# V of an attention layer by 20 products with 171-column blocks in place of seven Strassen products

## The chip, the core and the metric

One Trainium2 chip, one of its cores. The time is device microseconds of one launch of the whole program; the time of a kernel is the median of several runs.

## What is computed

The input `x` is 128 graphs of 128 nodes with 512 features, in f32. Layer 0 mixes the nodes of each graph by `adj`, takes a row maximum, adds it to `x` and normalises. Layer 1 is masked attention with 8 heads of 64 columns, a projection, and two normalisations. What matters here is the part of layer 1 ahead of the attention:

```python
def _L1_gnn_ref(x, w_qkv, w_proj, b_proj, ln_gamma, ln_beta, attn_mask):
    ...
    qkv = (x @ w_qkv).reshape(b, n, 3, H, hd).transpose(2, 0, 3, 1, 4)
    q, k, v = (qkv[0], qkv[1], qkv[2])
    attn = jnp.einsum('bhnd,bhmd->bhnm', q, k) * scale
    attn = jnp.where(attn_mask[None, None] == 0, -jnp.inf, attn)
    attn = jax.nn.softmax(attn, axis=-1)
    o = jnp.einsum('bhnm,bhmd->bhnd', attn, v).transpose(0, 2, 1, 3).reshape(b, n, d)
    o = o @ w_proj + b_proj
    ...
```

So V is `x` (all tokens by 512) times the last 512 columns of `w_qkv` (512 by 512), and everything stays in f32.

## The kernel before

**Groups and steps.** Four graphs make a group, 512 tokens; there are 32 groups and one step of the main loop (L1353) for each. The step of group p attends the group before (A: `attend`, L1153), forms scores and softmax of group p (S: L1030 and L1049), V of group p (V), the projection of group p-1 (O: `o_unit`, L1001), layer 0 of group p+2 (L: `l0_mm`, L474), and Q and K of group p+1 (Q: `Bilinear`, L799). The order of TensorE's pieces in a step is written out by hand in three lists: `FIRST` (L140) for the first step, `STEP` (L134) for the 30 in the middle, `LAST` (L146) for the last. `V5` in a list is product 5 of V, `Q17` is node 17 of Q and K, and so on. In the first step I, J, X and D stand for layer 0 of groups 0 and 1, transposes on TensorE, and Q and K of group 0 by plain products (`qk_plain`, L745). In the last step B, T and R attend, finish and project what is left.

**The other engines.** Every piece of work is an `Op` with a cost, an engine and the buffers it reads and writes. `Plan.run` (L212) keeps TensorE's order as the lists have it, and sorts the work of VectorE (DVE), ScalarE (ACT), GpSimd (POOL) and the DMA queue of SyncE (SP) by the time at which TensorE will want it. Each engine then executes its own queue strictly in that order.

**Q and K** are not formed by plain products. `token_sums` (L777) makes 18 sums of the eight token blocks `x1T` (each 128 features by 256 tokens) on POOL, into nine buffers `hl0` to `hl8`. `weight_forms` (L683) makes 26 sums of blocks of the weights once, at the start, on DVE and ACT. `Bilinear.node` (L823) walks a table: a node adds one or two products into a PSUM bank, and the bank is then handed on to a later node (chain), copied by ACT into another bank that a later node goes on with (a seed, L844), copied by ACT to an SBUF buffer `u` for later use (L847), or combined on DVE, and on POOL for a second summand, into a block of the result. One product of Q and K is two matmuls that stream 256 columns, and each f32 matmul is two MATMUL instructions in the profile.

**V and the projection** use Strassen's method with seven products on 2 by 2 blocks (`Strassen`, L901). A product is four matmuls of 256 columns, that is eight MATMUL instructions in the profile; seven products are 56. For V, `v_unit` (L967) makes four token sums on POOL per group (`unit_sums`, L985, into `hl0` to `hl3`), takes three ACT copies of the accumulating bank (`snap`, L936) and four DVE additions that write the result (`result`, L938). The weights of V need four sums on POOL at the start (`weight_sums(wv)`, L1418).

**PSUM** has eight banks, handed out first in, first out (`take`, L358).

The three places where the list sets V among the rest are these:

```python
STEP = """
A0 A1 A2 A3 S0 S1 S2 S3 V1 V2 L0 L1 V6 V5 O1 O2 V7 L3 L2 V4 O6 V3 O5 O7 O4 Q0 O3 Q2 Q3 Q1 Q4 Q5 Q6
Q7 Q8 Q9 Q10 Q11 Q12 Q13 Q14 Q15 Q17 Q16 Q19 Q20 Q18 Q21 Q22 Q24 Q25 Q23
""".split()
LAST = """
A0 A1 S0 A2 S1 A3 V1 S2 S3 O1 V5 V6 V4 O5 O2 V7 O6 O7 O4 T3 V3 V2 B0 B1 O3 T2 T1 T0 R0 R1 B2 B3 R3
R2
""".split()
```

Of the kernel before, what the change touches and what calls it, by code (L numbers as in the profile page):

```python
# [14 lines left out]
AX = mybir.AxisListType  # L15

# [24 lines left out]
TEMPS = [  # L41
    (10, 13, 1),
    (3, 10, 1),
    (0, 3, -1),
    (4, 7, -1),
    (4, 5, 1),
    (13, 14, -1),
    (9, 17, -1),
    (2, 3, 1),
    (11, 16, 1),  # L50
]
FORMS = [
    ((10, -1), (14, -1)),
    ((19, -1),),
    ((16, 1),),
    ((4, -1), (16, 1)),
    ((3, -1),),
    ((4, -1), (17, 1)),
    ((13, -1),),
    ((3, 1), (12, 1), (16, 1)),  # L60
    ((19, 1), (21, -1)),
    ((17, -1),),
    ((16, -1), (18, 1)),
    ((2, 1), (10, -1)),
    ((12, -1), (24, -1)),
    ((10, 1), (11, 1)),
    ((6, 1), (7, 1), (23, -1)),
    ((0, 1), (22, 1)),
    ((12, 1), (15, -1), (21, 1)),
    ((8, -1), (11, 1), (18, 1)),  # L70
    ((20, -1), (23, 1)),
    ((9, -1), (10, 1)),
    ((15, -1), (19, 1), (24, -1)),
    ((20, -1),),
    ((1, 1), (2, -1), (18, 1)),
    ((1, 1), (20, -1), (22, -1)),
    ((5, 1), (6, -1), (21, 1)),
    ((8, -1), (9, -1), (12, -1), (13, -1)),
]


NODES = [
    (((8, 0),), 3, (2,), (), None),
    (((12, 1),), 6, (), (19,), None),
    (((14, 2),), 4, (8,), (), None),
    (((1, 3), (10, 4)), 5, (), (7,), None),
    (((5, 5), (15, 6)), 9, (7,), (), None),
    (((9, 7),), 25, (10,), (), None),
    (((11, 8),), 14, (12,), (), None),
    (((17, 9),), 11, (20,), (), None),  # L90
    (((13, 10),), 13, (), (16,), None),
    (((16, 11),), 17, (), (12,), None),
    (((18, 12),), 19, (), (11,), None),
    (((19, 13),), 16, (), (15,), None),
    (((5, 14),), None, (), (), 6),
    (((20, 15),), 23, (18,), (), None),
    (((7, 16),), 15, (), (19,), None),
    ((), None, (), (), 7),
    (((6, 17),), None, (), (), 4),
    (((21, 18),), 21, (), (24,), None),  # L100
    (((22, 19),), 22, (), (25,), None),
    (((23, 20),), None, (), (), 3),
    (((24, 21),), 24, (), (22,), None),
    (((0, 22),), None, (), (23, 22), None),
    ((), None, (), (), 1),
    (((25, 23),), None, (), (), 5),
    (((1, 24),), None, (), (), 2),
    (((2, 25),), None, (), (), 0),
]
SIGN = [1, 1, 1, -1, -1, -1, -1, -1, 1, 1, -1, -1, 1, 1, -1, -1, -1, 1, 1, -1, -1, 1, -1, -1, -1, -1]  # L110

EDGES = {
    0: {3: -1, 2: 1},
    1: {19: 1, 6: -1},
    2: {8: 1, 4: -1},
    3: {7: -1, 5: 1},
    4: {7: 1, 9: -1},
    5: {10: 1, 25: 1},
    6: {12: -1, 14: 1},
    7: {11: 1, 20: 1},  # L120
    8: {16: 1, 13: 1},
    9: {12: 1, 17: 1},
    10: {19: 1, 11: 1},
    11: {16: 1, 15: 1},
    13: {18: 1, 23: -1},
    14: {19: 1, 15: 1},
    17: {24: 1, 21: 1},
    18: {25: 1, 22: -1},
    20: {24: 1, 22: 1},
    21: {23: 1, 22: 1},  # L130
}
# [3 lines left out]
A0 A1 A2 A3 S0 S1 S2 S3 V1 V2 L0 L1 V6 V5 O1 O2 V7 L3 L2 V4 O6 V3 O5 O7 O4 Q0 O3 Q2 Q3 Q1 Q4 Q5 Q6  # L135
Q7 Q8 Q9 Q10 Q11 Q12 Q13 Q14 Q15 Q17 Q16 Q19 Q20 Q18 Q21 Q22 Q24 Q25 Q23
# [4 lines left out]
K1 I0 K1 I1 I2 J0 K1 J1 I3 X0 X1 J2 D0 X2 D1 J3 X3 D3 D2 D6 D4 S1 S0 D5 D7 V1 V4 L0 L1 S3 V6 V5 L2  # L141
V7 V2 V3 Q0 Q1 S2 L3 Q2 Q3 Q4 Q5 Q8 Q9 Q6 Q17 Q10 Q7 Q12 Q14 Q21 Q13 Q11 Q19 Q20 Q23 Q18 Q15 Q24 Q25
Q16 Q22
# [3 lines left out]
A0 A1 S0 A2 S1 A3 V1 S2 S3 O1 V5 V6 V4 O5 O2 V7 O6 O7 O4 T3 V3 V2 B0 B1 O3 T2 T1 T0 R0 R1 B2 B3 R3  # L147
R2
# [162 lines left out]
def kernel(  # L311
# [19 lines left out]
    HE = D // 2  # L331
    NG = B // G
# [23 lines left out]
    free = deque(range(8))  # L356

    def take():  # L358
        return bank(free.popleft())
# [319 lines left out]
    def block(i):  # L679
        k, n = divmod(i, 4)  # L680
        return raw[n], None, lambda: raw[n].t[:, k]

    def weight_forms():  # L683
        made = {}
        temp_bufs = [buf(s, [P, 4, HE]) for s in ("z", "xr0", "xr1")]

        def operand(i):
            if i < 16:
                return block(i)
            i -= 16  # L690
            b, c = temp_bufs[i // 4], i % 4
            return b, c, lambda: b.t[:, c]

        def add(dst, dst_at, a, b, sa, sb_):
            (ba, ka, pa), (bb, kb, pb) = a, b
            reads = [(ba, ka), (bb, kb)]
            if sa < 0 and sb_ < 0:
                plan.add(
                    "DVE",
                    0.62,  # L700
                    lambda: stt(dst(), pa(), -1.0, pb(), ALU.mult, ALU.subtract),
                    reads,
                    [dst_at],
                    both=True,
                )
                return
# [3 lines left out]
            plan.add("DVE", 0.49, lambda: tt(V, dst(), pa(), pb(), op), reads, [dst_at], both=True)  # L710

        def temp(i):
            if i in made:
                return
            made[i] = True
            a, b, s = TEMPS[i]
            for o in (a, b):
                if o >= 16:
                    temp(o - 16)
            bt, c = temp_bufs[i // 4], i % 4  # L720
            add(lambda: bt.t[:, c], (bt, c), operand(a), operand(b), 1, s)

        for w, terms in enumerate(FORMS):
            for i, _ in terms:
                if i >= 16:
                    temp(i - 16)
            form, at = (lambda w=w: wqk.t[:, w]), (wqk, w)
# [14 lines left out]
            for i, s in terms[2:]:  # L742
                add(form, at, (wqk, w, form), operand(i), 1, s)
# [55 lines left out]
    class Bilinear:  # L799


        def __init__(self, g):
            self.g, self.left = g, lefts.pop(g)
            self.rooms = deque(f"u{i}" for i in range(6))
            self.banks, self.snaps = {}, {}

        def product(self, b, tok, w, start):
            bt, key, ap = self.left[tok]

            def emit():  # L810
                for s in range(2):
                    mm(halves(b)[:, s], wqk.t[:, w, ts(s, P)], ap(), start and s == 0)

            plan.add("PE", 0.862, emit, [(wqk, w), (bt, key)], [b])

        def place(self, block):
            h, c = divmod(block, 4)
            if (self.g, h) not in qk:
                qk[self.g, h] = buf(f"qk{h}", [P, 4, 2, HT])
            dst = qk[self.g, h]  # L820
            return dst, c, lambda: dst.t[:, c].rearrange("p k n -> p (k n)")

        def node(self, n):  # L823
            prods, chain, seeds, adds, block = NODES[n]
            fresh = n not in self.banks
            b = take() if fresh else self.banks.pop(n)
# [4 lines left out]
            for y in [y for y in self.snaps if n in self.snaps[y][1]]:  # L831
                u, users = self.snaps[y]
                users.discard(n)
                mine.append((u, SIGN[n] * EDGES[y][n] * SIGN[y]))
# [3 lines left out]
            if block is None:  # L838
                for u, s in mine:
                    op = ALU.add if s > 0 else ALU.subtract  # L840
                    plan.add("DVE", 0.62, lambda u=u, op=op: tt(V, b.t, b.t, u.t, op), [u, b], [b])
                for m in seeds:
                    nb = self.banks[m] = take()
                    plan.add("ACT", 0.5, lambda nb=nb: pin(A.copy(nb.t, b.t)), [b], [nb])  # L844
# [626 lines left out]
```

## Time and profile before

| what | value |
|---|---|
| median of 3 runs | 1882.04 us (1880.76 to 1882.06) |
| the profiled execution's own time | 1882.49 us |
| its span, first to last instruction | 1879.6 us |
| busy: TensorE matmul (PE) | 1863.4 us, 11293 instructions |
| busy: TensorE weight load (PEld) | 1594.2 us |
| busy: DVE, ACT, POOL | 1323.9, 1475.6, 1542.1 us |
| DMA | 341.88 MB, mean 182 GB/s |

The profile lists for each engine how long it was busy. A matmul stands in it twice, as a weight load (LDWEIGHTS on PEld) and as a MATMUL on PE; successive MATMULs overlap in the records, so the distance from one start to the next is the cost of one and not its duration. In the timeline and the groups "k" is a PSUM bank, "wv" and "wqk" are the weights of V and of Q and K, "wp" those of the projection, "hl" and "x1T" token sums and token blocks, "so" the token sums of the projection, "u" the copies. A number in brackets at the end of a timeline row is the time for which the engine stood idle before it, with what released it.

### The profile page before, as it was taken

To read this page: it belongs to the slowest core of one execution; us is meant where nothing else is said; L and a number is where in the kernel's file an instruction comes from. 1 tells how busy PE (TensorE), PEld (TensorE's weight loads), DVE (VectorE), ACT (ScalarE), POOL (GpSimd) and SP (SyncE) were. 2 spreads that over 40 slices of the span, in tenths; PEclk is the share of its full clock that TensorE was granted. 3 is DMA by queue.
4 is the path that set the end of the run, shared out by engine and by line. 5 is a ranking of instruction groups with operands and counts; after the bars stand their busy time and mean duration, and the time that the engine had idled before them with its cause. 6 is when DMAs were issued, how large, how long until landed. Compare 5 with 4: busy or idle time off the path is not lost.

```text
span 1879.6 us, 35324 instructions
## 1 busy us (share of the span) xinstructions
PE 1863.4 (99%) x11293; PEld 1594.2 (85%) x11293; DVE 1323.9 (70%) x2433; ACT 1475.6 (79%) x4376; POOL 1542.1 (82%) x1598
## 2 busy tenths in 40 slices
PE   9999999999999999999999999999999999999997
PEld 7788888888888888888888888888888888888884
DVE  8977676676766677667767667676677676677667
ACT  2787777987778877779777788777887777987785
POOL 5678988889888889888898888888888988889884
PEclk9999999999999999999999999999999999999999
DMA  7764676556676556766566765667655677656654
GB/s 220 198 169 128 188 194 198 171 168 182 180 217 181 165 168 189 203 189 171 168 188 183 220 167 167 168 189 214 184 167 165 190 192 196 173 172 177 180 191 146
DMA packets 444888, 341.88 MB, mean 182 GB/s; under 512 B 276768, under 2 KB 378272, under 8 KB 444704
## 3 DMA queue, kind: packets, MB, share of 16 engines
q1 hardware_dynamic: 444416, 339.11, 63.9%
q8 instruction: 90, 1.47, 0.3%
q14 instruction: 94, 0.77, 0.1%
q10 hardware_dynamic: 288, 0.52, 0.1%
HBM read 172.82 MB, written 166.72 MB: 181 GB/s over the span
## 4 chain that ended last, share of the span: by engine, by line
PE 96%; DVE 2%; POOL 1%; issue 0%; ACT 0%; POOLq 0%; DVEq 0%; ACTq 0%
PE k L380 96%; DVE wqk L374 1%; DVE st L497 0%; POOL hl L374 0%; POOL z L374 0%; DVE xr L374 0%; POOL rs L374 0%; DVE z L374 0%; DVE s L377 0%; POOL o L374 0%; DVE qk L771 0%; PE k L642 0%; DVE z L377 0%; DVE nm L1075 0%; POOL wp L374 0%
## 5 line engine op out<-in xcount | busy, mean ns | idle before, releaser
L380 PE MATMUL k<-hl,wqk 128*128 128x256 f32 x2232 | 522.4, 380 | 0.6 <-ACT k L844 0.4
L380 PEld LDWEIGHTS k<-hl,wqk 128*128 128x128 f32 x2232 | 424.6, 190 | 58.7 <-issue 1.2
L1084 ACT ACTIVATE s<-s,nm 128x128 f32<-128x128 f32 x1024 | 395.9, 390 | 7.8 <-DVE nm L1075 7.8
L1113 ACT ACTIVATE s<-s,rec 128x128 f32<-128x128 f32 x992 | 306.3, 391 | 0.0
L377 DVE SCALAR_TENSOR_TENSOR qk<-k,u 128x512 f32<-128x512 f32 x248 | 169.7, 686 | 109.3 <-PE k L380 55.9
L380 PE MATMUL k<-x1T,wqk 128*128 128x256 f32 x992 | 244.5, 380 | 0.0
L374 POOL TENSOR_TENSOR hl<-x1T 128x512 f32<-128x512 f32 (+1 forms) x250 | 216.4, 871 | 33.3 <-PE k L380 33.3
L847 ACT COPY u<-k 128x512 f32<-128x512 f32 x341 | 192.2, 581 | 60.6 <-PE k L380 33.3
L380 PE MATMUL k<-wv,hl 128*128 128x256 f32 x1024 | 237.0, 380 | 1.9 <-POOL hl L374 1.0
L380 PE MATMUL k<-wp,so 128*128 128x256 f32 x992 | 229.7, 380 | 0.7 <-ACT u L936 0.7
L380 PEld LDWEIGHTS k<-wv,hl 128*128 128x128 f32 x1024 | 194.7, 190 | 41.6 <-issue 8.7
L380 PEld LDWEIGHTS k<-wp,so 128*128 128x128 f32 x992 | 188.6, 190 | 26.5 <-ACT u L936 1.1
L380 PEld LDWEIGHTS k<-x1T,wqk 128*128 128x128 f32 x992 | 188.7, 190 | 25.6 <-DVE wqk L374 0.3
L377 DVE SCALAR_TENSOR_TENSOR s<-k,mask 128x512 f32<-128x512 f32 x256 | 156.5, 681 | 72.8 <-PE k L380 72.8
L374 POOL TENSOR_TENSOR hl<-x1T,hl 128x512 f32<-128x512 f32 (+1 forms) x249 | 196.0, 803 | 0.1
L1084 ACT ACTIVATION_READ_ACCUMULATOR s<-s,nm 128x1 f32 x1024 | 193.7, 189 | 0.0
L1125 DVE STREAM_TRANSPOSE pu<-s 128x1024 f32<-128x1024 f32 x128 | 158.2, 1236 | 37.5 <-ACT s L1113 36.4
L380 PE MATMUL k<-wv,x1T 128*128 128x256 f32 x768 | 179.6, 384 | 0.0
L380 PEld LDWEIGHTS k<-wv,x1T 128*128 128x128 f32 x768 | 143.6, 190 | 34.1 <-issue 14.0
L380 PE MATMUL k<-wp,oT 128*128 128x256 f32 x744 | 171.0, 380 | 0.0
L1174 ACT COPY oT<-k 128x512 f32<-128x512 f32 x128 | 75.0, 586 | 118.8 <-PE k L380 118.6
L374 POOL TENSOR_TENSOR x<-x,be_bc 128x1024 f32<-128x1024 f32 x62 | 146.3, 2360 | 19.0 <-ACT xr L568 13.1
(140 smaller groups left out, 3401.7 us busy)
## 6 DMA issues: line engine op xcount, KB each, us to landing
hop<-pu SPq DMA_DIRECT2D x128, 512.0 KB, 2.9
s<-hop SPq DMA_DIRECT2D x512, 128.0 KB, 3.6
xhop<-xt SPq DMA_DIRECT2D x248, 128.0 KB, 3.8
spill<-x SPq DMA_DIRECT2D x62, 512.0 KB, 4.5
x1T<-xhop SPq DMA_DIRECT2D x248, 128.0 KB, 4.6
x<-in_x_dram SPq DMA_DIRECT2D x60, 512.0 KB, 5.0
xr<-spill SPq DMA_DIRECT2D x60, 512.0 KB, 5.1
out_dram<-xr SPq DMA_DIRECT2D x60, 512.0 KB, 4.1
```

The costliest lines, as they stand in the source:

```text
L374: pin(eng.tensor_tensor(dst, a, b, op))
L377: pin(V.scalar_tensor_tensor(dst, a, s, b, op0, op1))
L380: pin(PE.matmul(dst, lhsT=lhsT, rhs=rhs, start=start, stop=True, skip_group_check=True))
L847: plan.add("ACT", 0.5, lambda: pin(A.copy(u.t, b.t)), [b], [u])
L1084: A.activation(flat()[:, i], flat()[:, i], AF.Exp, bias=nm.t[:, i : i + 1], accum_out=sm.t[:, i : i + 1],)
L1113: A.activation(flat()[:, i], flat()[:, i], AF.Identity, scale=rec.t[:, i : i + 1])
L1125: V.transpose(u.t.rearrange("p q h b -> p h q b"), flat().rearrange("p h (q a) -> p h q a", q=Q),)
L1174: lambda: pin(A.copy(dst.t[:, :, ts(jj, P)], bk.t.rearrange("p (c n) -> p c n", c=KC))),
```

## The change

V is formed as Q and K are, from a second table. The result (two blocks of 256 tokens by three blocks of 171 columns, 512 rounded up to 513) is made of 20 products of a token sum and a weight form, in 18 nodes. The token sums are those that `token_sums` made for Q and K of the same group one step earlier; no sums are made for V. The token sum is now the stationary operand and the weight form of 171 columns the one that streams, so a product is two matmuls of 171 columns. The forms of V's weights (8 shared sums, then 20 forms: 12 of one term, 6 of two, 2 of three) are made once, at the start, behind those of Q and K, in the slots of temporary buffers; the raw weights of V lie in the slot of `wp`, so the projection's weights are loaded, and summed on POOL, after V of the first group. V of that first group is formed by plain products (P): four pieces of four matmuls of 512 columns. In the last step the `u` copies of V are made on DVE and not on ACT. The projection is unchanged. All three lists are new.

```diff
+VV = Table(
+    12,
...
+    [
+        (((18, 0),), 4, (3,), (), None),
+        (((21, 1),), 9, (), (8,), None),
+        (((0, 2),), 7, (5,), (), None),
+        (((6, 3),), 6, (), (17,), None),
+        (((7, 4),), 10, (8,), (), None),
+        (((20, 5),), 16, (), (6,), None),
+        (((25, 6),), None, (), (8, 13), None),
+        (((2, 7),), 11, (12,), (), None),
+        (((5, 8),), None, (), (), 4),
+        (((9, 9), (17, 10)), 13, (), (11,), None),
+        (((11, 11),), 15, (14,), (), None),
+        (((24, 12),), None, (), (), 0),
+        (((23, 13),), None, (), (16, 15), None),
+        (((19, 14),), None, (), (), 3),
+        (((14, 15), (13, 16)), 17, (), (16,), None),
+        (((1, 17),), None, (), (), 1),
+        (((22, 18),), None, (), (), 2),
+        (((12, 19),), None, (), (), 5),
+    ],
...
 STEP = """
-A0 A1 A2 A3 S0 S1 S2 S3 V1 V2 L0 L1 V6 V5 O1 O2 V7 L3 L2 V4 O6 V3 O5 O7 O4 Q0 O3 Q2 Q3 Q1 Q4 Q5 Q6
-Q7 Q8 Q9 Q10 Q11 Q12 Q13 Q14 Q15 Q17 Q16 Q19 Q20 Q18 Q21 Q22 Q24 Q25 Q23
+A0 A1 A2 A3 S0 S1 S2 S3 V0 V1 V2 V3 V4 V5 V6 V7 V8 V9 V11 V10 V12 V13 V14 V15 L1 V16 V17 L0 O1 O2 O6
+O5 O7 O4 Q0 L3 L2 O3 Q2 Q3 Q1 Q4 Q5 Q6 Q7 Q8 Q9 Q14 Q10 Q11 Q12 Q15 Q13 Q17 Q19 Q20 Q18 Q21 Q23 Q22
+Q24 Q16 Q25
...
 FIRST = """
-K1 I0 K1 I1 I2 J0 K1 J1 I3 X0 X1 J2 D0 X2 D1 J3 X3 D3 D2 D6 D4 S1 S0 D5 D7 V1 V4 L0 L1 S3 V6 V5 L2
-V7 V2 V3 Q0 Q1 S2 L3 Q2 Q3 Q4 Q5 Q8 Q9 Q6 Q17 Q10 Q7 Q12 Q14 Q21 Q13 Q11 Q19 Q20 Q23 Q18 Q15 Q24 Q25
-Q16 Q22
+K1 K1 K1 I0 I1 I2 J0 I3 J1 X0 X1 J2 X2 D0 X3 D3 D4 D5 D7 D6 D1 D2 J3 S3 L2 L3 P2 S2 S1 P0 P1 P3 Q0
+S0 Q2 Q1 Q3 Q4 Q6 L1 Q9 Q8 Q7 Q5 Q12 Q14 Q17 Q10 Q21 Q13 Q11 Q19 L0 Q23 Q18 Q20 Q16 Q25 Q24 Q22 Q15
...
 LAST = """
-A0 A1 S0 A2 S1 A3 V1 S2 S3 O1 V5 V6 V4 O5 O2 V7 O6 O7 O4 T3 V3 V2 B0 B1 O3 T2 T1 T0 R0 R1 B2 B3 R3
-R2
+A2 V0 A0 A1 V2 V3 S0 V5 V1 A3 V6 S1 V4 S2 V7 V8 V10 V9 V11 V14 V13 O1 V12 O2 V16 O6 S3 O5 O7 V17 V15
+O4 O3 B0 B1 T3 R0 B2 T1 R2 T0 B3 R1 T2 R3
...
             def emit():
                 for s in range(2):
-                    mm(halves(b)[:, s], wqk.t[:, w, ts(s, P)], ap(), start and s == 0)
+                    dst = b.t[:, ts(s, width)]
+                    if width == HT:
+                        mm(dst, form.t[:, w, ts(s, P)], ap(), start and s == 0)
+                    else:
+                        mm(dst, ap()[:, ts(s, P)], form.t[:, w], start and s == 0)
...
                 for m in seeds:
-                    nb = self.banks[m] = take()
-                    plan.add("ACT", 0.5, lambda nb=nb: pin(A.copy(nb.t, b.t)), [b], [nb])
+                    nb = self.banks[m] = take(2 * width, True)
+                    plan.add("ACT", act, lambda nb=nb: pin(A.copy(cols(nb), cols(b))), [b], [nb])
                 if adds:
                     u = buf(self.rooms.popleft(), [P, 512])
-                    plan.add("ACT", 0.5, lambda: pin(A.copy(u.t, b.t)), [b], [u])
+                    if self.on_vector:
+                        plan.add("DVE", dve, lambda: pin(V.tensor_copy(cols(u), cols(b))), [b], [u])
+                    else:
+                        plan.add("ACT", act, lambda: pin(A.copy(cols(u), cols(b))), [b], [u])
...
+    def v_unit(g):
+        def out(i):
+            h, c = divmod(i, 3)
+            if (g, h) not in vs:
+                vs[g, h] = buf(f"v{h}", [P, 2, 3 * VB])
+            dst = vs[g, h]
+            return dst, c, lambda: dst.t[:, :, ts(c, VB)]
+
+        costs = (0.58, 0.42, 0.46, 0.87)
+        return Bilinear(VV, lefts.pop(g), wv, VB, ["u0", "u1", "u2"], costs, out, g == NG - 1)
+
+    def v_plain(n):
+        h, j = divmod(n, 2)
+        xT = x1T[0]
+        if j == 0:
+            vs[0, h] = buf(f"v{h}", [P, 2, 3 * VB])
+        v, b = vs[0, h], take()
+
+        def emit():
+            for k in range(KC):
+                mm(b.t, xT.t[:, h, k, ts(j, P)], wv_raw.t[:, k, :D], k == 0)
+
+        plan.add("PE", 3.45, emit, [wv_raw, (xT, h)], [b])
+        plan.add("ACT", 0.5, lambda: pin(A.copy(v.t[:, j, :D], b.t)), [b], [(v, j)])
+        give(b)
...
-                weight_forms()
-                weight_load(wp, w_proj, 0)
+                weight_forms(QK, wqk, HE, qk_block, ("z", "xr0", "xr1"), 0.49)
+                weight_forms(VV, wv, VB, v_block, ("z", "xr0"), 0.37)
...
-                weight_sums(wv)
-                weight_sums(wp)
...
+            if p == 0 and i == last["P"]:
+                wp = buf("wp", [P, 7, 2, HE])
+                weight_load(wp, w_proj, 0)
+                weight_sums(wp)
```

`take` now also gives a 342-column product a bank whose upper columns are stale, and keeps such banks from full-width accumulation onto a copy; it changes which bank is used and adds no instruction.

## The prediction

> **What bounds the kernel now.** I first read the page: the busy line and the chain of work that ended last.
>
> ```profile
> PE 1863.4 (99%) x11293; PEld 1594.2 (85%) x11293; DVE 1323.9 (70%) x2433; ACT 1475.6 (79%) x4376; POOL 1542.1 (82%) x1598
> ...
> PE 96%; DVE 2%; POOL 1%; issue 0%; ACT 0%; POOLq 0%; DVEq 0%; ACTq 0%
> ```
>
> TensorE is the bound: it is idle for 16.2 us of 1879.6, and in the chain it holds one piece from 61.56 to 1799.5 us without a break. So a change is worth what it does to the length of TensorE's list, plus the waits that it makes or takes away. The length is read from the PE timeline of one middle step: from one row's start to the next, over the instructions of the row.
>
> ```profile
> 1011.07 3.71 PE L380 MATMUL k<-s,v 128*64 128x128 f32 x64
> 1014.71 3.84 PE L380 MATMUL k<-qk 64*128 64x128 f32 x64
> 1018.48 3.72 PE L380 MATMUL k<-wv,x1T 128*128 128x256 f32 x16
> 1022.04 1.88 PE L380 MATMUL k<-x,adjT 128*128 128x512 f32 x4
> 1023.76 3.62 PE L380 MATMUL k<-wv,hl 128*128 128x256 f32 x16
> 1027.21 3.62 PE L380 MATMUL k<-wp,oT 128*128 128x256 f32 x16
> 1030.66 1.89 PE L380 MATMUL k<-wv,hl 128*128 128x256 f32 x8
> ```
>
> One MATMUL of 256 columns takes (1030.66-1027.21)/16 = 215.6 ns, one of 512 (1023.76-1022.04)/4 = 430 ns. For 128 columns on the full array there are the transposes of the first microseconds: (12.31-11.43)/8 = 110 ns.
>
> ```profile
> 11.43 1.04 PE L642 MATMUL k<-ident,x 128*128 128x128 f32 x8
> 12.31 1.02 PE L380 MATMUL k<-o,adjT 128*128 128x512 f32 x2
> ```
>
> **The price of 171 columns.** No row shows it. The line through 256 and 512 gives 215.6-85x0.8375 = 144.4 ns, the one through 128 and 256 gives 110+43x0.825 = 145.5. I take 145. It holds if the weight load, one for each MATMUL, stays hidden. That is the point to look at, since a load is recorded as longer than that:
>
> ```profile
> L380 PEld LDWEIGHTS k<-wv,hl 128*128 128x128 f32 x1024 | 194.7, 190 | 41.6 <-issue 8.7 <-ACT s L1084 5.7 <-POOL hl L374 1.4
> ...
> L380 PEld LDWEIGHTS k<-qk 64*128 64x128 f32 x2048 | 117.1, 188 | 7.2 <-issue 6.3 <-DVE st L497 0.8 <-DVE mvz L498 0.2
> L380 PEld LDWEIGHTS k<-s,v 128*64 128x64 f32 x2048 | 111.1, 137 | 12.7 <-issue 10.4 <-DVE v L374 1.4 <-DVE qk L377 0.7
> ...
> L642 PEld LDWEIGHTS k<-ident,x 128*128 128x128 f32 x16 | 1.9, 141 | 1.1 <-issue 0.8 <-ACT x L568 0.2
> ```
>
> 190 ns is a latency, by three rows: 128 weight columns take 190, 64 take 137, so a column costs 0.83 ns and 128 cost 106, the rest overlapping; the scores (k<-qk, 188 ns) go at 3.77/64 = 59 ns, two halves of the array side by side, so each half takes a load in every 118 ns; and the transposes' loads of 141 ns go at 110. Bounds: 144 at best; 190 if full-array loads of this kind cannot overlap each other. I take 145, as both neighbouring shapes lie on one line.
>
> Here a rule speaks against the change. The Trainium skill, "TensorE: Matmul & The Clock Gate", section "Back-to-back issue gap", says that in a stream of load and matmul pairs both set the spacing: about 81 ns at 128 columns, where the matmul alone would be 56. Taking those 25 ns on top (an estimate from that page), a MATMUL of 171 columns would be 170 ns, V 13.6 us a group, and the kernel about 48 us slower. The 110 ns of the transposes carry no such surcharge, and the sum below goes by the rows.
>
> **V in groups 1 to 31.** Removed: 56 MATMULs x 215.6 = 12.07 us a group. Added: 20 products x 2 matmuls x 2 = 80 MATMULs x 145 = 11.60. That is -0.47 x 31 = **-14.6 us**. Per unit it is thin: a pitch of 150 would undo it.
>
> **V of group 0.** 32 MATMULs of 512 columns x 430 = 13.76 for 12.07: **+1.7 us**.
>
> **The other engines in a middle step** (busy in one period, 1011.07 to 1068.74):
>
> ```profile
> 1011.07:1068.74 57.67, 57.67 (x354) 49.69 (x354) 40.01 (x74) 46.54 (x138) 48.63 (x50) 1.00 0.66 180
> ```
>
> In order: PE, PEld, DVE, ACT, POOL. ACT loses 3 copies x 585 ns and gains 12 of 342 columns (5 seeds, 7 u); a copy takes 374 (256 columns) to 581 (512), so by the line 444: +3.6, to 50.1 of 57.2 us. DVE loses 4 x 684 and gains 7 x about 510 (between 422 and 686): +0.8. POOL loses four sums x 1280 and gains two second summands x about 915 (between 731 and 1276): -3.3. No engine gets longer than TensorE; hidden behind its 57.2 us, they cost nothing in sum. What can cost is latency, since ACT now stands in V's chain. A product waits until the bank that it goes on with is seeded. From the end of a product to the copy's start ACT takes 0.2 us, and from the copy's end to TensorE 0.06, by these rows of the last step (the product of 1838.23 ends at 1839.96):
>
> ```profile
> 1838.23 1.89 PE L380 MATMUL k<-wp,so 128*128 128x256 f32 x8
> 1840.79 2.00 PE L380 MATMUL k<-wp,so 128*128 128x256 f32 x8 [0.67 <-ACT u L936]
> ...
> 1840.15 0.58 ACT L936 COPY u<-k 128x512 f32<-128x512 f32 x1
> ```
>
> So the loop is 0.2+0.44+0.06 = 0.7 us. The tightest places (V0 to V3, V2 to V5, V10 to V14, and V3 to V6 through its u copy) leave two products, 1.16 us: 0.46 spare. What may stand before a copy in ACT's queue is one exponential (0.39 us) or one normalisation (0.81). In ACT's new order the first six copies stand together directly behind the four oT copies, where ACT now idles 4.3 us, since the exponentials need DVE's maxima; only later are exponentials and two normalisations among them, and the products that wait for those copies lie three or more further on, but for V14. If V0's copy slips, what is queued behind it is u of V1 and the seed of V5, then the exponentials. Banks: V takes the banks of S0 to S2, which DVE empties 0.61 us apart from 1.2 us after the first score; the fifth is free 4.3 us after it, and V5's seed wants it at 5.7. Bounds for these waits 0 to 0.3 us a step; a wait that ends just in time still shows a load (about 0.1 us in rows such as 1018.48, where 3.56 us stand for 16 x 215.6 = 3.45). I take 0.07 x 30 = **+2 us** (0 to +9).
>
> **Token sums.** Those for Q and K now wait until V has read them (V17, at about 12.3 us after the scores), not until the Strassen sums of V are read (V3, at 25.9), and Q0 follows 11 us after V17. That covers the 13 us of sums, since hl0 is free after V9. L2 and L3, moved past Q0, feed only the step after next: cover of tens of us. Costed at nothing; if the cover went, one sum, 0.73 us, a step.
>
> **Start.** The four POOL sums of V's weights (wv, 5.5 us) and the four token sums go out of POOL's queue, and these idle times of the first group's V with them:
>
> ```profile
> 51.78 3.69 PE L380 MATMUL k<-wv,hl 128*128 128x256 f32 x16 [0.42 <-ACT u L936]
> ...
> 56.81 1.99 PE L380 MATMUL k<-wv,hl 128*128 128x256 f32 x8 [0.48 <-ACT u L936]
> ...
> 61.56 1.97 PE L380 MATMUL k<-wv,hl 128*128 128x256 f32 x8 [1.03 <-POOL hl L374]
> ```
>
> 1.9 us could go; the next to be late are Q's first nodes, behind 18 DVE instructions for V's forms (0.3 to 1.5 us each by the wqk rows, 5 to 27 us, wanted only at about 95 us) and wp's load and sums, which now stand behind P and are wanted at about 107 (its four DMAs, issued from 14.30 to 17.6 us now, leave SP's queue ahead of the transposes of group 1, and come back in it behind them, where 40 us cover 3.3). I take **-1 us** (-2 to +3).
>
> **End.** V's results no longer hold up the last attends (1.03 us at 1849.00, 0.67 at 1840.79). But S3 is moved: between it and B3 stand four O (6.9), V17 and V15 (1.2), three B (2.7) and two R (6.9) = 17.7 us, where 32 stood. Its softmax needs mask 1.5, maximum 1.2, exponentials 3.1, reciprocal 0.4, scaling 2.4, transpose 1.4, and two DMA hops with five issues, about 8.4: 18.4, with no queueing. I take a wait of 2 to 3 there, less 1.7: **+1 us** (-2 to +4).
>
> **Sum.** -14.6+1.7+2-1+1 = -10.9. The profiled execution took 1882.49, 0.45 above the median; 1882.04-10.9 = **1871**, its own range 1866 to 1877.
>
> **Rivals.**
> (a) The gain is eaten: 148 to 150 ns a MATMUL (3 to 5 ns of the pairs' overhead; scores and attends go at 118 and 114 a pair, 4 to 8 above the transposes), or 0.2 to 0.4 us of waits a step. For it: 10.9 is the difference of two large terms. Against it: the shapes beside it lie on a line. 1877 to 1884.
> (b) ACT's seeds are late. Three tight seeds, each by one exponential beyond its spare, 0.3 us: 0.9 x 31 = 28, so about 1899. It turns the sign from 0.42 us a step. Against it: the order of ACT, and the Q products, whose seeds wait without idle time (though three to four times as far apart in time).
> (c) The load sets the pace: 190 ns, V 15.2 us, +3.1 x 31+1.7 = 98, so about 1980; from 150 ns on it is slower. Against it stand 110 and 118 ns.
>
> **Numbers.** Forecast 0.66, (a) 0.18, (b) 0.12, (c) 0.04. Within 0.2% (3.8 us, about what a measurement of this kernel can tell from no change) falls half of (a), 0.09; faster are the forecast and the other half, 0.75; slower (b) and (c), 0.16. The range 1865 to 1884 leaves out (b), (c) and a little below.
>
> **What would show it.** Rows k<-hl,wv and k<-x1T,wv with 171 columns at 0.145 us (0.58 a product); a step of about 57.2 us; no idle bracket "ACT k" in V; brackets before the first Q nodes, and before B3 in the last 20 us. A pitch above 150, or ACT brackets in every step, would make the forecast wrong.

## The result, and the profile after

The changed kernel takes 1878.55 us (median of 19 runs, 1876.01 to 1879.84); the kernel before, run beside it, 1881.69 (19 runs, 1880.76 to 1883.14). The ratio is 0.9982, with a 95% interval of 0.9975 to 0.9989: 3.1 us or 0.18% faster. The forecast was 1871. The profiled execution of the changed kernel took 1876.14 us (span 1874.3), 2.4 below its median, so the traces show 5.3 us of span and not 3.1; what follows accounts for those 5.3.

First the page of the changed kernel: its busy line and the chain of work that ended last.

```profile
PE 1854.3 (99%) x12013; PEld 1620.4 (86%) x12013; DVE 1374.6 (73%) x2547; ACT 1576.1 (84%) x4661; POOL 1427.9 (76%) x1529
...
PE 96%; DVE 2%; DMA 1%; ACT 1%; POOL 1%; issue 0%; POOLq 0%; ACTq 0%; DVEq 0%
```

ACT went from 1475.6 to 1576.1 us, DVE from 1323.9 to 1374.6, POOL from 1542.1 to 1427.9. TensorE is still the bound, and idle for 20.0 us where it was idle for 16.2. So it was not the pieces that grew, but the waits. Next a middle step on TensorE, as it was shown of before (start, duration, instruction, count).

```profile
1018.60 1.33 PE L466 MATMUL k<-wv,hl 128*128 128x171 f32 x8
1019.76 1.32 PE L466 MATMUL k<-wv,x1T 128*128 128x171 f32 x8
1020.92 4.82 PE L466 MATMUL k<-wv,hl 128*128 128x171 f32 x32
```

From 1018.60 to 1020.92 stand 16 MATMULs of 171 columns: 2.32/16 = 145 ns each, the price that the forecast took. No bracket stands in the step. The row of the same step in the table by stretches (length, then PE, PEld, DVE, ACT, POOL, granted clock, DMA share, GB/s) shows TensorE busy for all of it:

```profile
1008.16:1065.38 57.22, 57.22 (x377) 50.60 (x376) 41.67 (x77) 49.82 (x149) 45.38 (x48) 1.00 0.65 184
```

It was 57.67 before. Where the rest went is read by cutting the span at the start of each step's first attend:

| stretch | before | after | difference |
|---|---|---|---|
| first step, 0 to the first attend | 88.40 | 86.67 | -1.73 |
| step 1 | 57.67 | 63.25 | +5.58 |
| steps 2 to 29, together | 1614.66 | 1602.11 | -12.55 (28 steps, 0.45 each) |
| step 30 | 55.27 | 57.88 | +2.61 |
| last stretch | 63.60 | 64.37 | +0.77 |

The waits of TensorE by what ended them (total, times, longest) name the two steps that lost:

```profile
PE k L466 <- DVE s L463: 3.2, 1, 3.2
PE k L466 <- ACT k L939: 2.6, 2, 1.9
```

The first is one wait, for a mask (`s`, L463) that DVE lays on the scores of step 1. TensorE at that place:

```profile
90.32 3.84 PE L466 MATMUL k<-qk 64*128 64x128 f32 x64
97.38 2.65 PE L466 MATMUL k<-wv,hl 128*128 128x171 f32 x8 [3.22 <-DVE s L463]
99.82 3.47 PE L466 MATMUL k<-wv,x1T 128*128 128x171 f32 x12
103.13 1.33 PE L466 MATMUL k<-wv,hl 128*128 128x171 f32 x8
```

V's first node wants a PSUM bank in which scores still lie until DVE has masked them. Eight MATMULs then take 2.44 us (99.82-97.38), 305 ns each, the next twelve 276, and only from 103.13 on is it 145 again. The table by stretches gives the granted clock of that time as 0.67 (it is 1.00 in the same 9 us of the kernel before):

```profile
97.00:106.00 9.00, 8.62 (x40) 8.62 (x41) 9.00 (x15) 3.15 (x8) 2.36 (x1) 0.67 0.45 116
```

So step 1 loses 3.2 in the wait and (2.44-8x0.145)+(3.31-12x0.145) = 2.85 in the clock, 6.0 in all, which is what it stands above 57.22. The Trainium skill, "TensorE: Matmul & The Clock Gate", section "What's actually happening", has the clock halved after at least one idle window of about 3.4 us, in a count that runs freely. The half speed agrees with this trace; the length does not quite: the wait here is 3.2 us, and in the profiled executions of e2, e7, e8, e11 and e12 the clock fell behind a wait of 1.89 us too.

What DVE did meanwhile is in its timeline:

```profile
89.29 2.13 DVE L460 TENSOR_TENSOR wv<-wp,xr 128x171 f32<-128x171 f32 x1
91.35 1.40 DVE L463 SCALAR_TENSOR_TENSOR wv<-wp,z 128x171 f32<-128x171 f32 x1
...
95.31 1.42 DVE L460 TENSOR_TENSOR z<-wp,z 128x171 f32<-128x171 f32 x1
96.65 4.26 DVE L463 SCALAR_TENSOR_TENSOR s<-k,mask 128x512 f32<-128x512 f32 x7
```

Five of the 18 sums for V's weights (`wv`, `z`) stand in front of the masks, 89.29 to 96.65. And they are slow: the same instruction took 0.33 us at 77 to 82 us. POOL's timeline shows what differs:

```profile
88.87 2.36 POOL L460 TENSOR_TENSOR x<-x,be_bc 128x1024 f32<-128x1024 f32 x1 [2.69 <-DVE xt L689]
91.19 1.37 POOL L460 TENSOR_TENSOR so<-oT 128x512 f32<-128x512 f32 x1
```

DVE's first sum ends at 91.42, as POOL's addition does (91.23), the second at 92.75, as POOL's next (92.56): one for each.

### The profile page after: what moved, and what is told of

It is laid out like the page before. It is cut to its first block, busy times and chain, and to the rows that moved or that the text cites. A ratio compares the mean times of both kernels' runs of the same rounds, so it can differ in the third digit from the quotient of the medians.

```text
span 1874.3 us, 37519 instructions
## 1 busy us (share of the span) xinstructions
PE 1854.3 (99%) x12013; PEld 1620.4 (86%) x12013; DVE 1374.6 (73%) x2547; ACT 1576.1 (84%) x4661; POOL 1427.9 (76%) x1529
## 4 chain that ended last, share of the span: by engine, by line
PE 96%; DVE 2%; DMA 1%; ACT 1%; POOL 1%; issue 0%; POOLq 0%; ACTq 0%; DVEq 0%
PE k L466 96%; DMA xr<-spill 0%; DVE st L583 0%; ACT s L1202 0%; DMA spill<-x 0%; DMA out_dram<-xr 0%; POOL wqk L460 0%; DVE qk L463 0%; POOL rs L460 0%; ACT xr L654 0%; POOL x L460 0%; ACT k L939 0%; DVE k L463 0%; DVE x L460 0%; DVE wqk L460 0%
## 5 line engine op out<-in xcount | busy, mean ns | idle before, releaser
L1231 ACT ACTIVATE s<-s,rec 128x128 f32<-128x128 f32 x992 | 316.2, 392 | 0.0
L945 ACT COPY u<-k 128x512 f32<-128x512 f32 x551 | 283.6, 528 | 36.0 <-PE k L466 26.4
L939 ACT COPY k<-k 128x512 f32<-128x512 f32 x372 | 191.6, 516 | 137.1 <-PE k L466 125.2
L466 PE MATMUL k<-wv,hl 128*128 128x171 f32 x1736 | 277.9, 310 | 3.2 <-DVE s L463 3.2
L466 PEld LDWEIGHTS k<-wv,hl 128*128 128x128 f32 x1736 | 259.3, 190 | 21.5 <-issue 14.3
L463 DVE SCALAR_TENSOR_TENSOR qk<-k,u 128x512 f32<-128x512 f32 x248 | 169.2, 685 | 100.0 <-ACT u L945 51.6
L466 PE MATMUL k<-wp,so 128*128 128x256 f32 x992 | 224.5, 379 | 0.0
L463 DVE SCALAR_TENSOR_TENSOR s<-k,mask 128x512 f32<-128x512 f32 x256 | 156.7, 680 | 75.1 <-PE k L466 75.1
L460 POOL TENSOR_TENSOR z<-z,ga_bc 128x1024 f32<-128x1024 f32 x60 | 142.1, 2368 | 40.1 <-ACT z L654 37.0
L466 PEld LDWEIGHTS k<-wp,oT 128*128 128x128 f32 x744 | 141.1, 190 | 31.5 <-issue 6.9
L460 POOL TENSOR_TENSOR hl<-x1T,hl 128x256 f32<-128x256 f32 x217 | 157.0, 737 | 0.6 <-PE k L466 0.4
L1193 DVE TENSOR_REDUCE nm<-s 128x8 f32<-128x1024 f32 x128 | 151.8, 1204 | 0.1
```

Of the source, the lines that this page charges most:

```text
L460: pin(eng.tensor_tensor(dst, a, b, op))
L463: pin(V.scalar_tensor_tensor(dst, a, s, b, op0, op1))
L466: pin(PE.matmul(dst, lhsT=lhsT, rhs=rhs, start=start, stop=True, skip_group_check=True))
L939: plan.add("ACT", act, lambda nb=nb: pin(A.copy(cols(nb), cols(b))), [b], [nb])
L945: plan.add("ACT", act, lambda: pin(A.copy(cols(u), cols(b))), [b], [u])
L1193: lambda: pin(V.tensor_reduce(nm.t, flat(), AX.X, ALU.max, negate=True)),
```

## The experiments

The theory after the result: **step 1 loses 6.0 us to V's weight sums on DVE, slowed by POOL and placed ahead of the masks; step 30 loses 3 because ACT, which took over V's copies, is its bound.** The rivals: in step 1 it is the clock, the new list or a wait for something else; in step 30 a chain behind DVE or POOL. All runs in one table (times in us; the ratio is to the kernel before; stretches from the profiled execution; e4 and e8, one execution each, add work in front, so their whole time is not compared):

| run | median | ratio [95%] | step 1 | step 30 | last stretch |
|---|---|---|---|---|---|
| changed kernel | 1878.55 | 0.9982 [0.9975, 0.9989] | 63.25 | 57.88 | 64.37 |
| e1_no_v_sums | 1870.07 | 0.9937 [0.9924, 0.9951] | 57.22 | 56.96 | 64.26 |
| e2_fill | 1876.65 | 0.9976 [0.9966, 0.9985] | 62.52 | 59.57 | 64.35 |
| e5_pool_forms | 1870.96 | 0.9943 [0.9929, 0.9956] | 57.22 | 56.98 | 64.27 |
| e7_quiet_pool | 1896.35 | 1.0086 [1.0071, 1.0102] | 57.22 | 59.23 | 65.61 |
| e3_scale30_dve | 1877.61 | 0.9979 [0.9970, 0.9988] | 63.38 | 53.95 | 69.04 |
| e6_both | 1875.42 | 0.9966 [0.9953, 0.9978] | 57.63 | 53.96 | 72.36 |
| e9_pool_s3 | 1872.17 | 0.9948 [0.9931, 0.9964] | 57.22 | 56.12 | 66.14 |
| e10_pool_u30 | 1874.25 | 0.9962 [0.9947, 0.9976] | 57.22 | 60.27 | 65.19 |
| e11_price | 1897.91 | 1.0081 [1.0064, 1.0097] | 60.08 | 59.23 | 65.51 |
| e12_u_act | 1880.40 | 0.9993 [0.9983, 1.0003] | 62.11 | 59.57 | 68.31 |
| e4_stream | 1921.38 | | 57.22 | 56.95 | 65.17 |
| e8_dve_stream | 1915.63 | | 57.44 | 59.39 | 65.39 |

**e1_no_v_sums.** V's forms of two and three terms become one raw block each; the 18 sums on DVE are left out.

```diff
+            if table is VV and len(terms) > 1:
+                terms = ((w % table.blocks, 1),)
```

> The changed kernel with V's weight forms of two and three terms replaced by a scaled copy of one raw block on ScalarE, so 18 VectorE sums of the start are left out (V of groups 1 to 31 is not the reference's). Theory (the forms stand in VectorE's queue ahead of the masks of step 1's scores, and TensorE waits there): the 3.2 us wait at V0 of step 1 goes, and the slow stretch behind it, so step 1 takes 57.2 to 57.6 us where it took 63.25, and the profiled span is about 6 us shorter (1868). Rival (step 1 is late for another reason: transfers of the projection's weights, the spill, the token sums): step 1 stays above 61 us.

Measured: 1870.07; step 1 takes 57.22, the length of every other middle step. The masks start as soon as the scores are there, 92.01 us in this row of DVE:

```profile
92.01 4.28 DVE L463 SCALAR_TENSOR_TENSOR s<-k,mask 128x512 f32<-128x512 f32 x7 [3.11 <-PE k L466]
```

So the sums make the whole excess of step 1, not the new list or the copies.

**e2_fill.** TensorE gets work in the place of the wait: the last graph's scores of step 1 are formed four times, so that it does not fall idle.

```diff
+        again = 4 if b == 7 else 1
```

> The changed kernel with the eight matmuls of S3 in step 1 issued four times over, with the same result, 2.8 us of TensorE work just where it waits for VectorE. Theory (the wait costs twice: 3.4 us of idle time, and 2.85 us after it because the granted clock falls): V's first 20 MATMULs of step 1 go at 145 ns where they went at 276 to 305, the granted clock of that stretch stays near 1.00 where it was 0.67, and step 1 takes about 60.4 us where it took 63.25. Rival (V is slow there because its own weight forms are not ready): the pitch stays near 290 ns with short waits on VectorE, and step 1 stays at 63.

Measured: 1876.65; the clock stays at 1.00 from 97 to 106 us and V's MATMULs take 145 ns. But step 1 falls only to 62.52, where 60.4 was expected: the filler itself takes 2.8 us, and behind it stand waits of 0.55, 0.35 and 0.64 us.

```profile
98.64 1.45 PE L466 MATMUL k<-wv,hl 128*128 128x171 f32 x8 [0.55 <-DVE s L463]
...
108.65 2.15 PE L466 MATMUL k<-wv,hl 128*128 128x171 f32 x12 [0.64 <-ACT u L945]
```

The clock did fall because of the idle time, but its 2.85 us had covered lateness that shows once TensorE runs at full speed. Of the price of step 1 most is DVE's lateness either way.

**e5_pool_forms.** V's sums go to POOL, nothing else.

```diff
+            if table is VV:
+                plan.add("POOL", 0.5, lambda: tt(GP, dst(), pa(), pb(), op), reads, [dst_at])
+                return
             plan.add("DVE", cost, lambda: tt(V, dst(), pa(), pb(), op), reads, [dst_at], both=True)
```

> The changed kernel with V's weight sums on GpSimd (planned at 0.5 us each) and not on VectorE; the one form of two negative terms stays on VectorE. Theory: the wait at V0 of step 1 goes, step 1 takes 57.2 to 58 us, the median falls by about 6 us, to 1872 to 1873. Rival (what matters is the port that both engines share, not VectorE's queue): GpSimd's sums hold up VectorE's own sums for Q and K instead, Q0 to Q25 of step 0 wait, and step 0 and 1 together gain less than 2 us.

Measured: 1870.96, and step 1 at 57.22. POOL does the sums between 71 and 88 us, at 0.48 to 0.65 us each, in time that it had free. Of the kernels that leave nothing out it has the lowest median, and it is faster than both that this study began with.

**e7_quiet_pool.** The sums stay on DVE, and POOL is kept quiet beside them: the addition of beta for group 2 and the token sums of group 0's projection are left out.

```diff
-        left = unit_sums(a, s)
+        left = unit_sums(a, s) if g else {...}   # raw blocks
...
+        if q not in (4, 5):
             plan.add("POOL", 2.34, ...)
```

> V's weight sums stay on DVE, ahead of the masks; GpSimd is kept quiet beside them: the addition of beta for group 2 and the four token sums of group 0's projection are left out (raw blocks stand in for the sums; the output of those groups is not the reference's). Theory: the sums of 171 columns take 1.40 us only because GpSimd adds at the same time (0.33 at 76-82 us, when it doesn't); then the five sums at 89-97 us take about 2 us in place of 7.4, the masks start at about 91 us, TensorE's wait of 3.2 us at 97 us falls below 0.5, its clock stays at 1.00, and step 1 takes 57.2 to 58: 1872 to 1873.5 us. Rival: the place in DVE's queue alone is what costs (or the sums are slow for another reason): a wait of 2 to 3 us stays, 1876 to 1878.5.

Measured in step 1: as the theory has it. The five sums that took 7.4 us take 1.2 (89.58 to 90.78), the masks start on time, and step 1 is 57.22 with no wait (DVE's timeline):

```profile
89.58 0.29 DVE L460 TENSOR_TENSOR wv<-wp,xr 128x171 f32<-128x171 f32 x1
...
90.53 0.33 DVE L460 TENSOR_TENSOR z<-wp,z 128x171 f32<-128x171 f32 x1
...
92.75 4.28 DVE L463 SCALAR_TENSOR_TENSOR s<-k,mask 128x512 f32<-128x512 f32 x7 [1.40 <-PE k L466]
```

The place in the queue is the same; so what turns it into a wait is POOL. The total, 1896.35, is a miss of both theories: steps 3 to 29, whose work is untouched, take 57.2 to 61.8 us. That is taken up at e11.

**e8_dve_stream.** The price by itself, at the front of the changed kernel.

```diff
+    plan.add("DVE", 4, sums, [sa], [(sa, "d")])        # 12 x tensor_tensor, SBUF and SBUF
+    plan.add("DVE", 4, psum_sums, [sa], [pk])          # 12 x tensor_tensor, PSUM and SBUF
+    plan.add("DVE", 3, copies_, [sa], [(sa, "d")])     # 12 x tensor_copy in SBUF
+    plan.add("POOL", 30, pool_sums, ...)               # 24 x tensor_tensor of 512 columns
...                                                     # the three DVE series again, and 12 sums more
```

> The price by itself: at the front of the changed kernel DVE runs 12 sums of 171 columns from SBUF, 12 sums with one operand in PSUM, 12 copies in SBUF, first alone and then the same beside 24 sums of 512 columns on GpSimd, and 12 sums alone once more. Theory: two SBUF operands are what collides: 0.25-0.33 us a sum alone, 1.35-1.40 beside GpSimd; with an operand in PSUM, and for copies, no difference (0.25-0.30 and 0.15-0.25). Rival 1: everything on DVE slows beside GpSimd. Rival 2: nothing does, and the 1.40 us have another cause. GpSimd's own sums, 1.26-1.37 us in the trace, are expected at 1.27 either way.

Measured: POOL's sums ran first, from 2.05 to 28.8 us, so the rows with POOL are the early ones of DVE:

```profile
1.57 11.78 DVE L460 TENSOR_TENSOR u<-u 128x171 f32<-128x171 f32 x12
13.28 4.50 DVE L460 TENSOR_TENSOR k<-k,u 128x171 f32<-128x171 f32 x12
...
17.89 11.57 DVE L504 COPY u<-u 128x171 f32<-128x171 f32 x12
...
29.98 4.40 DVE L460 TENSOR_TENSOR u<-u 128x171 f32<-128x171 f32 x12
...
44.59 3.35 DVE L504 COPY u<-u 128x171 f32<-128x171 f32 x12
```

Two operands in SBUF: 0.37 us a sum alone, 1.115 from start to start beside POOL (from the third on; the first two of the row started before POOL's first), and POOL's own sums also start every 1.115. With one operand in PSUM there is no difference (0.375 by the row, and as much from 39.81 us on, without POOL). A copy within SBUF, expected to be free of it, is not: 0.28 alone, 1.115 beside POOL (but for the first and the last two of its row). So what collides is a DVE sum of two SBUF operands, or a copy within SBUF, and it goes at one DVE instruction for each POOL instruction, whether it takes 0.37 or 0.28 us alone. Not all that DVE does within SBUF collides: in the changed kernel's middle steps the transpose of 1024 columns (`pu<-s`) takes 1.25 us and the maximum over 1024 (`nm<-s`) 1.21, beside POOL's sums and without them. The Trainium skill, "SBUF — State Buffer", section "SBUF: two separate sides", gives a cause: the two engines share a pair of SBUF ports, taken by one of them for a whole instruction, for DVE's with two SBUF inputs or in a two-port mode. The rows of sums and copies agree. In e5 the same sums on POOL cost 0.48 to 0.65 us each.

**e4_stream.** TensorE's price by width: streams of matmuls on zeros at the front of the changed kernel.

```diff
+    for n, cols in ((24, 256), (24, 171), (24, 128), (24, 96), (24, 64), (24, 171), (24, 256)):
+        stream(n, cols)
```

> The changed kernel with a stream of matmuls of zeros set in front: 24 each of 256, 171, 128, 96, 64, 171 and 256 columns, each with its own load of 128 weight columns. Theory (a load streams in 106 ns and the rest of its 190 ns overlaps): 216, 145, 109, then a floor near 107 to 110 for 96 and 64 columns, since the load sets the pace. Rival one (190 ns is the pace of loads): 216, 190, 190, 190, 190. Rival two (a load adds about 25 ns to each matmul): 216 to 240, 170, 135. Rival three (loads overlap altogether): 216, 145, 109, 82, 56.

Measured from start to start: 216 ns for 256 columns, 145 for 171, 112 for 128, for 96 and for 64. So a load-and-matmul pair of this kind has a floor of 112 ns, and 171 columns lie above it: the load stays hidden, as the rows of the transposes had said. This run and e8 also bear on step 1. With 51 us added in front, all 18 of V's sums, still on DVE, are done at 31.3 us, 111 us ahead of the masks of step 1, and the step takes 57.22. In e8, with 40 us added, the last sum ends as the first mask starts (133.1), and the step takes 57.44.

**e3_scale30_dve.** In step 30 two graphs' softmax scalings go from ACT to DVE.

```diff
-softmax(a + n, scores(a + n), p == 0 and n >= 2 or p == NG - 1 and n < 2)
+softmax(a + n, scores(a + n), p == 0 and n >= 2 or p >= NG - 2 and n < 2)
```

> Alone on the changed kernel: in step 30 the softmax scalings of two of the four graphs go from ACT (16 x 0.30 = 4.9 us) to DVE (2 x 1.55 us). Theory: step 30 lost 2.6 us because ACT, which idles no more from 1773 to 1804 us there, reaches the seeds of Q late; with 4.9 us less on ACT the step goes from 57.88 to 54.8-55.5 us, the waits for ACT's k copies at 1792 and 1804 us vanish, and the whole takes 1875.5 to 1876.5 us. Rival: ACT is only the last in a chain that begins with DVE's maxima or POOL's sums; then the step stays at 57.5 us or more and the time at 1878.5, or goes up, since DVE gets 3.1 us more.

Measured: step 30 falls to 53.95, below what was expected, and TensorE has no wait in it. So ACT was its bound. In the changed kernel ACT's queue shows it: a seed (`k<-k`, L939) that TensorE waits 1.89 us for stands behind seven scalings, and ahead of these stood two norms of 1.53 us together.

```profile
1801.77 2.16 ACT L1231 ACTIVATE s<-s,rec 128x128 f32<-128x128 f32 x7
1803.82 0.60 ACT L939 COPY k<-k 128x512 f32<-128x512 f32 x1
```

But the last stretch grows by 4.7 us and takes it back: waits of 1.17 (for V's u copy on DVE) and 1.56 (for a seed on ACT), and 13.4 us behind the last matmul where there were 11.1. The whole is 1877.61.

**e6_both**, e5 and e3 together.

> V's weight sums on GpSimd (as in e5_pool_forms, 1870.96 us) and the two scalings of step 30 on DVE. If the two losses are separate, the gains add: step 1 at 57.2 us, step 30 at 54.8-55.5 us in place of 56.98, the whole 1869.0 to 1869.8 us. Rival: step 30 is not held by ACT, and the time stays at 1871.

Measured: 1875.42, slower than e5 alone. The first half adds (step 1 at 57.63, step 30 at 53.96), the last stretch grows to 72.36. Neither expectation held.

**e9_pool_s3** and **e10_pool_u30**, both on e5: the scalings of one graph only, and V's u copies of step 30 on DVE.

```diff
 e9:  ... or p == NG - 1 and n < 2 or p == NG - 2 and n == 3)
 e10: return Bilinear(VV, lefts.pop(g), wv, VB, ["u0", "u1", "u2"], costs, out, g >= NG - 2)
```

> V's weight sums on GpSimd (e5_pool_forms: 1870.96 us, step 30 at 56.98, last stretch 64.27) and the scalings of one graph of step 30, the fourth, on DVE: 2.4 us less on ACT, 1.55 more on DVE. In e3 and e6 two graphs' scalings on DVE cut step 30 to 53.95, but the last stretch grew by 4.7 and 8.1. If the last stretch grows because DVE has more to do there, half the shift costs half of it or less: step 30 at 54.5 to 55.5, the last stretch at 64.3 to 66, the whole 1868.5 to 1871. If instead the last stretch grows because it now starts earlier than its own chains (V's u copies, ACT's seeds, the last tails) allow, the sum of the two stays at 121 us or more: 1871 to 1874.

> V's weight sums on GpSimd (e5_pool_forms) and V's seven u copies of step 30 on DVE, as in the last step: 3.1 us less on ACT, 3.6 more on DVE, early in the step (DVE is busy 16.2 of 20 us there). If ACT's total decides step 30, it goes from 56.98 to 54.5-55.5 us. If what decides is what stands in ACT's queue directly ahead of Q's seeds (scalings, norms) from 1790 us on, it changes by less than 0.5 us, since ACT idles between V's copies anyway; then 1870.5 to 1871.5. As in e9, an earlier end of step 30 may be given back in the last stretch.

Measured: 1872.17 and 1874.25. In e9 step 30 and the last stretch together are 122.3, in e5 121.25, in e3 123.0, in e6 126.3: the second reading of e9's expectation held, the end does not come earlier. In e10 step 30 became longer (60.27), with a wait of 2.27 us for a u copy on ACT in Q and 1.44 for POOL, which neither reading had. Behind the wait of 2.27 the clock falls once more: the next 12 MATMULs of 256 columns take 4.31 us in place of 2.59. So ACT's total does not decide step 30: e10 takes about as much from it there as e9 does (3.3 and 3.4 us), and the step grows. Taking away the scalings, which stand ahead of the seeds, shortens it (e3, e9), but that only moves the lateness on to the last stretch.

**e12_u_act.** One part of the change undone: the last step's u copies of V on ACT again.

```diff
-        return Bilinear(VV, ..., costs, out, g == NG - 1)
+        return Bilinear(VV, ..., costs, out)
```

> One part of the change undone: in the last step V's seven u copies are on ACT again, not on DVE. The last stretch is 0.76 us longer than before the change (64.37 against 63.60), and 1.2 us of waits stand in it, 0.51 of them for a u copy on DVE. Theory: DVE, busy 32.7 of the 40 us from 1810 on and 15 of the last 15, is what the last stretch goes by; with 7 x 0.5 us off it the wait of 0.51 goes and the end comes up to 1 us earlier: last stretch 63.4 to 64.3, the whole 1877.5 to 1878.5. Rival: ACT (31 of the 40 us) has the softmax of the last graphs right behind these copies; then waits for ACT's u and k copies appear and the stretch is 65 to 68 us: 1879 to 1882. Steps 1 to 30 stay as in the changed kernel.

Measured: 1880.40 against 1878.55; last stretch 68.31. The rival's time held, not its mechanism: the only wait of that stretch is one of 1.82 us for ACT's `oT` copy, not for its u and k copies. The clock falls behind it (eight MATMULs of 512 columns take 5.32 us, where the changed kernel takes 3.63), and 12.8 us stand behind the last matmul where there were 11.1. So this part of the change is worth about 2 us; by which chain is not shown. (The profiled execution, 1884.19, was the slowest of its ten.) It also shows a middle step, 29, at 59.34, in a place where ACT's order is that of the changed kernel. TensorE waits 1.85 us there for V's u copy, and ACT's and POOL's rows show why:

```profile
1710.98 1.52 ACT L654 ACTIVATE z<-o,sh,rs 128x512 f32<-128x512 f32 x2 [2.21 <-POOL xr L460]
1712.40 0.42 ACT L945 COPY u<-k 128x342 f32<-128x342 f32 x1
```

```profile
1708.58 2.36 POOL L460 TENSOR_TENSOR xr<-xr,z 128x1024 f32<-128x1024 f32 x1 [3.48 <-DMA xr<-spill]
```

A reload from DRAM came late, POOL's addition waited for it, the norm on ACT waited for POOL, and V's copy stood behind the norm in ACT's queue.

**e11_price.** One number of the planner is altered: 1.4 us for a sum of V's weights in place of 0.37. The program's work is the same.

```diff
-                weight_forms(VV, wv, VB, v_block, ("z", "xr0"), 0.37)
+                weight_forms(VV, wv, VB, v_block, ("z", "xr0"), 1.4)
```

> The changed kernel with one number altered: the planner reckons 1.4 us for a sum of V's weights on DVE in place of 0.37. No work is added or taken away, only orders change. If the cause in step 1 is the planner's price, the sums spread out among the masks of step 1 and TensorE's wait of 3.2 us there breaks up into shorter ones: step 1 at 58.5 to 61 us, the whole 1874 to 1877. If it is the amount of work on DVE whatever its order, step 1 stays at 62 to 64. Beside that it is a control for e7_quiet_pool: there the middle steps lost 18 us though only work of step 0 and 1 was left out. If any new order of the queues can do that, middle steps here depart from 57.22 us as well; else they stay.

Measured: step 1 at 60.08, as the price theory had it, the one wait for a mask down to 1.5 us. But the whole is 1897.91: middle steps take 57.2 to 59.1 us, as in e7. Their TensorE work is unchanged; what changed is the order of the other queues. In a step of 59.07 us ACT's row is

```profile
1028.07 1.52 ACT L654 ACTIVATE z<-o,sh,rs 128x512 f32<-128x512 f32 x2 [1.16 <-POOL xr L460]
1029.50 0.42 ACT L945 COPY u<-k 128x342 f32<-128x342 f32 x1
```

and TensorE waits 0.81 us for that u copy. Both norms stand ahead of it and wait 1.16 us for POOL's addition. In the changed kernel's step from 1008.16 an exponential comes ahead of the first norm, a u copy and a seed of V stand between the two, and neither norm waits. e7 has the same order as e11 of ACT, DVE and POOL in a middle step (step 12 compared), and all other runs share the changed kernel's order of ACT. So the middle step's 57.22 is not the price of the change as such, but of the change in one order. The order is not all of it: from one middle step to the next it stays the same in e11, and the steps still take 57.2 to 59.1. What varies from step to step was not followed.

## Why the prediction was wrong, step by step

**What it got right.** The MATMUL of 171 columns: 145 ns, in the step and alone (e4); rival (c), the load that sets the pace, is refuted by it, and so is rival (a)'s 148 to 150; the time fell into (a)'s range, but by neither of its causes. A middle step: 57.22 against "about 57.2". Rival (b), late seeds in every step, did not come about in this order; its mechanism is real, as e11 and e12's step 29 show. The waits of the middle steps, put at 2 us, measured nothing in the profiled execution: 28 x 0.45 = 12.55 where the sum had 0.40 a step.

**Where it failed: "Start", -1 with a range of -2 to +3.** The step said that V's 18 DVE instructions take "5 to 27 us" and are "wanted only at about 95 us", and took Q's first nodes for the next to be late. It asked when the sums are wanted and not what stands behind them in the same queue. Wanted at 95, they were put just ahead of the masks that free V's banks; the masks came 5 us late (96.65 here, 91.57 in e5, with the attends at 86.7 in both), and step 1 cost 6.0 us. Removing the sums (e1), moving them (e5), and quieting POOL (e7) each brings the 57.22 back, and so does a start that leaves them time (e4). The total duration, 15 us, lay inside the stated range; but eleven of the 18 sums took about 0.33 us, and the five ahead of the masks 1.4 to 2.1. The reason was in the trace of before: there a sum of 256 columns takes 0.41 us at 82.52, where POOL is idle, and 2.22 at 80.37, beside a POOL addition of 2.36. What POOL did beside each was not looked up.

**In the same term, on the good side:** the first step is 1.73 shorter, where +1.7 for V in 512 columns and -1.9 for its waits would make -0.2. The distances from start to start around the three brackets, less the price of their MATMULs, held about 2.7 us, not the 1.9 that the brackets add up to: a bracket counts only from the modelled end of the last matmul. That more than pays for V's plain products; the rest, 0.7 us, is in the first 13 us and was not followed.

**A step that was not priced: step 30, +2.61 where -0.4 was due.** "No engine gets longer than TensorE; hidden behind its 57.2 us, they cost nothing in sum" holds for the steps with layer 0. Step 30 has none (the L's are dropped), its TensorE work is 53.95 us by e3, and ACT carries 48.2 there, with V's 3.1 us of u copies and 2.2 of seeds among them, and the scalings and norms late. e3 shows that ACT's scalings hold the step; that V's copies on ACT do is not shown, since e10 takes seven of them away and the step grows. e3, e6 and e9 show that the last stretch, in which DVE is busy 14.98 of the 15 us from 1850 on (13.96 before the change), is next. How the two last stretches could be made as short as before the change (118.87 against 121.25 in e5) stays open.

**"End", +1 (-2 to +4): +0.77, for another reason.** Its wait of 2 to 3 us ahead of B3 did not come: B3 starts at 1855.06 without a bracket. What grew is the stretch behind the last matmul, from 10.13 to 11.06 us. The wait of 1.03 for V's results went, as forecast.

Summed against the forecast of -10.9: 3.6 in the first step and step 1 (+4.3 measured, +0.7 forecast), 3.1 in step 30, -1.4 in the other middle steps, 0.2 at the end, 5.5; measured -5.3. With e5 in place of the change's own sums the time is 1870.96, but that it meets the 1871 is partly chance, since the first step's gain pays for step 30. The changed kernel's median is 2.4 above its profiled execution, while before it was below it. Step 30 holds most of an answer. TensorE at its wait of 1.89 us, in the changed kernel and then in e2:

```profile
1804.56 1.10 PE L466 MATMUL k<-hl,wqk 128*128 128x256 f32 x4 [1.89 <-ACT k L939]
1805.50 1.03 PE L466 MATMUL k<-x1T,wqk 128*128 128x256 f32 x4
```

```profile
1805.14 1.83 PE L466 MATMUL k<-hl,wqk 128*128 128x256 f32 x4 [1.89 <-ACT k L939]
1806.76 1.91 PE L466 MATMUL k<-x1T,wqk 128*128 128x256 f32 x4
```

Behind the same wait the clock fell in the profiled executions of e2, e7, e8, e11 and e12, whose step 30 takes 59.2 to 59.6 us, and not in the changed kernel's, with 57.88. If it falls in most executions of the changed kernel, that is 1.4 to 1.7 of the 2.4 us. e2's times part in the same way: three of 1878.35 to 1878.57 at a granted clock of 0.997, the profiled one among them, and six of 1875.77 to 1877.43 at 0.998. It stays an argument, since one execution of the changed kernel was profiled; the late reload in e12's step 29 is another candidate.

## What to carry to other kernels

Where work is moved to another engine's queue, ask not only when its result is wanted but what stands behind it there and who waits for that; one-time work at the start counts as much as that of a loop. Check "hidden behind the bound" in the stretch where the bound has least to do, here the step from which layer 0 was dropped. And a margin of 0.45 us a step belongs to an order as much as to a method: two kernels of equal middle work and another order (e7, e11) lost 21 and 15 us in steps 2 to 29 of their profiled executions.

## What the runs showed of the hardware

- A DVE sum of two SBUF operands, or a copy within SBUF, runs at POOL's pace while POOL adds: 1.115 us in place of 0.37 (sum) and 0.28 (copy) at 171 columns in e8; with an operand in PSUM nothing changes. POOL's pace in e8, 1.115, is the same beside either. In step 1 of the changed kernel POOL pays a little too: 1.36 to 1.37 us for a sum beside DVE's, 1.27 to 1.30 for the same sums in e5.
- A load-and-matmul pair on the full array in f32 takes at least 112 ns (64, 96 and 128 columns alike); 171 columns take 145, 256 take 216.
- After 3.2 us of idle time TensorE ran at half speed for about 5 us (305 ns in place of 145), which cost 2.85 us. Shorter waits did it in some runs: behind the 1.89 us of e2's step 30, four MATMULs of 256 columns took 1.62 us and the next four 1.71, in place of 0.86; behind the same wait in the changed kernel the first four took 0.94. Behind e3's wait of 1.56 us the clock did not fall.
